# The last 512 rows of a scan as two chunks of 256, with their operands made in one piece

## The chip, the core and the metric

The kernel runs on one core of one Trainium2 chip. The metric is the device time of one launch in microseconds (us), the median of several runs. Engines are named as in the profile: PE is TensorE (with its weight loads as PEld), DVE is VectorE, ACT is ScalarE, POOL is GpSimd, SP is SyncE, whose queue issues most of the DMAs.

## The reference, cut to what matters

One layer on 4096 rows of 256 values, all in float32: a selective scan (Mamba) block with residual and layer norm, then a mixture of experts with residual and layer norm.

```python
x_in, z = split(x @ W_in.T)                       # 512 + 512 channels
xc = silu(causal_conv(x_in, 4 taps) + b_conv)
dt = softplus(xc @ W_dt.T + b_dt)
Bm, Cm = xc @ W_B.T, xc @ W_C.T                   # 16 states each
h = exp(dt * A) * h + dt * Bm * xc                # along the rows; 512 channels x 16 states
y = sum over states of h * Cm
x = layernorm(x + (y * silu(z)) @ W_out.T)
p = softmax(x @ router.T)                         # 32 experts; the 6 best of p + bias, weights renormed
out = sum over 6 of weight * down_e(silu(gate_e(x)) * up_e(x)) + shared expert(x)
x = layernorm(x + out)
```

## The kernel before, in words

**Chunks.** The rows go through in chunks of T = 512 (`SIZES`, `AT`, line 91): eight of them. For each chunk c there are three parts. `front(c)` (line 867) makes the scan's operands: input projection, convolution, silu, dt, the B and C rows (written to DRAM as `bcd`), and u times dt; inside it `gate(c-1)` (line 983) makes z of the chunk before. The scan itself is the loop over `units` (line 1223). `tail(c)` (line 1023) transposes the gated y, multiplies by W_out, adds the residual row, does the layer norm and calls `prepare(c)` (line 284): router, softmax, six best, `ranked` (line 411: each row's place in expert order, and the list of full tiles), and the shared expert.

**A unit of the scan** is 128 channels x 512 rows of one state: `du_at` multiplies u by the broadcast B row (POOL, line 1121), `exp_at` makes exp(dt A) in PSUM (ACT, line 1132), the scan runs over it (DVE, line 1260), its result is multiplied by the broadcast C row (DVE, line 1267) and summed over states by transposing matmuls into y (PE, line 1178). `keep` saves the last column as the next chunk's start (ACT, line 1159). There are 64 units a chunk, 512 in all. `load_bc` (line 1081) broadcasts a B or C row over 128 partitions, 256 KB, for two units at a time; B rows have 3 buffers, C rows 4. The du of a unit is issued four units ahead of its scan, the exponential two.

The helpers already have a short form, which nothing used so far: for a chunk below 512 rows (`short`, line 1068) a unit holds two channel blocks of 256 rows side by side in one 128x512 tile. Then there are 32 units a chunk, two exponentials a unit, `joined` (line 1138) folds the second block's start into du and sets that column of h to zero, and the loop calls `step` twice a unit.

**Order of the work.** Everything but the units is a Python generator in `threads`; `step()` advances every thread by one yield, once a unit (line 1279). So the order of each engine's instructions, and of SP's DMAs, is written out when the kernel is built, and every engine keeps to it. At a chunk's first unit (line 1225) the loop starts the threads of that chunk: the tail of the chunk before, the front of the chunk after (or, in the last chunk, `last_gate` and `walls`), `blanked` (zero rows for tiles to come). PSUM banks are held by `room` and `free`.

**Rows to experts.** `copies` (line 537) scatters each row block of a chunk six times into the DRAM buffer `xs`, which is ordered by expert (POOL, line 552, indirect DMA): 24 scatters for a chunk of 512. Between two scatters that directly follow each other it puts a small memset (line 550); before chunk NC - 2 it spreads them out instead. The row buffer is single: `load_rows` (line 1010) of a chunk waits for the scatters of the chunk before. A pair of full tiles of 128 rows is taken by `tiles` (line 706) as soon as a chunk's rows are placed; `full` (line 113) tells how many tiles a chunk completes. Of chunks before NC - 2 (`stage`, line 745) a pair is "own": it loads its two experts' weights itself (`loaded`, line 588, and `pair`, line 674). The later pairs run in `through_all` (line 1293) with all 32 experts resident in `wall`, a buffer that the scan's operands use before. `walls` (line 796) fills it in four steps: 18 experts' space is free at once, 4 more when the last gate is done, 5 when the scan is, 5 when the last chunk's output projection is. No resident pair starts before all are there. Each tile's result is added to one of three DRAM accumulators by an accumulating indirect DMA (POOL, line 664). When all are added, `finish` (line 1339) loads the three, adds them, does the layer norm and stores.

112 tiles are done by own pairs and 112 by resident pairs; before, 24 of the latter belong to chunk 6 and 88 to chunk 7.

Of the kernel before, what the change touches and what calls it, by code (L numbers as in the profile page):

```python
# [10 lines left out]
AF = mybir.ActivationFunctionType  # L11
# [5 lines left out]
P = 128  # L17
T = 512
NB = T // P
# [41 lines left out]
def kernel(  # L61
# [20 lines left out]
    nc = tc.nc  # L82
    L, D = x.shape
# [4 lines left out]
    NS = a_log.shape[1]  # L88
    TAPS = w_conv.shape[1]
    H = TAPS - 1  # L90
    SIZES = [T] * (L // T)
    NC = len(SIZES)
    AT = [sum(SIZES[:c]) for c in range(NC + 1)]
    E = router_t.shape[1]
# [21 lines left out]
    def blocks(c):  # L116
        return SIZES[c] // P

# [37 lines left out]
    threads = []  # L156
# [586 lines left out]
            yield  # L743

    def stage(c):
        own = c < NC - 2
        return [(c, j, own) for j in range(full[c - 1] if c else 0, full[c], 2)]


# [28 lines left out]
    scratch = cut(M, T)  # L778
    xin = cut(M, H + T)

    odd = (NC - 1) % 2
    us, dts, xTs = [None, None], [None, None], [None, None]
    us[1 - odd], dts[1 - odd], xTs[1 - odd] = cut(M, T), cut(M, T), cut(KD, T)
    bc_all = cut(T)
# [6 lines left out]
    z_all = cut(NB, DI)  # L791
# [27 lines left out]
    with ExitStack() as c1:  # L819
# [6 lines left out]

        def load_x(c):

            t = scratch.rearrange("p m t -> p (m t)")[:, : blocks(c) * D]
            t = t.rearrange("p (b d) -> p b d", d=D)  # L830
            nc.sync.dma_start(
                t, x[AT[c] : AT[c] + SIZES[c], :].rearrange("(b p) d -> p b d", p=P)
            )
            x_in[c] = t

# [28 lines left out]
        xT_of, u_of, z_of, dt_of, bcd_of, y_of = {}, {}, {}, {}, {}, {}  # L864
        b_of, c_of, du_of, h_of, hc_of = {}, {}, {}, {}, {}

        def front(c, gap):

            nb, Tc = blocks(c), SIZES[c]
            xT = xTs[c % 2]  # L870
            xT_of[c] = xT

            def turned(k):
                yield from room()
                pt = bank(f"pxt_{c}_{k}")
                for b in range(nb):
                    nc.tensor.transpose(pt[:, ts(b, P)], x_in[c][:, b, ts(k, P)], ident)
                yield
                nc.scalar.copy(xT[:, k, :Tc], pt[:, :Tc])
                free()  # L880

            yield from beside([turned(k) for k in range(KD)], 1)
            if c:
                last = SIZES[c - 1]
                nc.gpsimd.tensor_copy(xin[:, :, 0:H], xin[:, :, last : last + H])
            yield
            u = us[c % 2][:, :, :Tc]
            u_of[c] = u

            def projected(m):  # L890
                yield from room()
                px = bank(f"px_{c}_{m}")[:, :Tc]
                for k in range(KD):
                    nc.tensor.matmul(
                        px, w_in[:, k, ts(m, P)], xT[:, k, :Tc],
                        start=(k == 0), stop=(k == KD - 1),
                    )
# [36 lines left out]
            e = scratch[:, :, :Tc]  # L934
            dt_of[c] = dt

            def stepped(m):
                yield from room()
                pd = bank(f"pd_{c}_{m}")[:, :Tc]
                for k in range(M):  # L940
                    nc.tensor.matmul(  # L941
                        pd, w_dt[:, k, ts(m, P)], u[:, k, :],
                        start=(k == 0), stop=(k == M - 1),
                    )
                yield
# [12 lines left out]

            yield
            bcd = dram.tile([2 * NS, T], F32, tag="bcd", name=f"bcd_{c}")[:, :Tc]  # L960
            nc.sync.dma_start(bcd, bc)
            bcd_of[c] = bcd
            yield from beside([stepped(m) for m in range(M)], gap)

            for two in range(0, M, 2):
                yield
                while held[0] > len(pools) - 2:
                    yield
                lns = [bank(f"ln_{c}_{m}")[:, :Tc] for m in (two, two + 1)]
                for m, ln in zip((two, two + 1), lns):  # L970
                    nc.scalar.activation(ln, e[:, m, :], AF.Ln, bias=1.0)
                yield
                for m, ln in zip((two, two + 1), lns):
                    yield
                    nc.vector.tensor_add(ln, ln, dt[:, m, :])
                    nc.vector.tensor_mul(u[:, m, :], u[:, m, :], ln)
                    nc.scalar.copy(dt[:, m, :], ln)
                    free()
            if c + 1 < NC:
                yield from rounds(4)  # L980
                load_x(c + 1)

        def gate(c):

            while c - 1 not in z_done and c:
                yield
            z = z_all[:, : blocks(c)]
            z_of[c] = z

            def projected(b):  # L990
                yield from room()
                pz = bank(f"pz_{c}_{b}")
                for k in range(KD):
                    nc.tensor.matmul(
                        pz, xT_of[c][:, k, ts(b, P)], w_in[:, k, DI:],
                        start=(k == 0), stop=(k == KD - 1),
                    )
                yield
                nc.scalar.copy(z[:, b, :], pz)
                free()  # L1000

            yield from beside([projected(b) for b in range(blocks(c))], 2)

        def last_gate():
            yield from gate(NC - 1)
            yield
            nc.scalar.activation(z_of[NC - 1], z_of[NC - 1], AF.Silu)
            gated.add(NC - 1)

        def load_rows(c):  # L1010

# [211 lines left out]
        for q, (c, g, s, i) in enumerate(units):  # L1223
            left[c] -= 1
            if g == 0 and s == 0 and i == 0:
                mains = []
                if c == 0:
                    mains.append(blanks)
                else:
                    mains.append(tail(c - 1))  # L1230
                if c == 1:
                    mains.append(cleared())
                if c + 1 < NC:
                    mains.append(front(c + 1, 3))
                else:
                    mains.append(last_gate())
                    last_tail = tail(c)
                    threads.append(last_tail)
                if 0 < c:
                    ahead = blanked(bound(c - 1), bound(c), c)  # L1240
                if c == 2:
                    rest = tiles([item for c in range(NC) for item in stage(c)])
                    threads.append(rest)
                if c == NC - 1:
                    threads.append(walls())
                threads.extend(mains)

            if q % 4 == 0 and 0 < c:
# [169 lines left out]
```

## Time and profile before

| | us |
|---|---|
| median of 3 runs | 1851.69 (1851.32 to 1852.23) |
| profiled execution: time, span | 1859.8, 1857.9 |
| first units of chunks 4 to 7, at about | 741, 937, 1130, 1321 |
| last scan of the last chunk ends | 1508.3 |
| last accumulate lands | 1803.6 |
| busy in the span: PE, DVE, ACT, POOL | 1359.2, 1399.4, 990.9, 1216.3 |
| moved by DMA | 355.40 MB, 191 GB/s |

Groups of instructions that the change or its working touches (mean ns of one): scan 1283 and multiply by C 692 on DVE; du 1390 on POOL; exponential 128x512 692, tanh 128x512 586 and 128x256 384, state copy 158 on ACT; scatter 1001 and accumulate 1561 on POOL. One table load of ACT takes 1283.

How to read it: the page lists groups as line, engine, operation, output<-input, shape, count, then busy time, mean, idle time before them and what ended it. A timeline lists single instructions. In the DMA part "q1" is what the hardware queues of SP carry and "q0" what POOL's indirect DMAs carry; the share is the time their packets took on 16 engines. Busy shares are averages over stages; the windows show one stage at a time.

### The profile page before, as it was taken

The page shows a single profiled execution, that of the slowest core. Times are in us where ns is not written, and L with a number is a line of the kernel's source. Part 1 is how long each engine was busy: PE and PEld are TensorE (multiplying, and loading weights), DVE is VectorE, ACT ScalarE, POOL GpSimd, SP SyncE. Part 2 cuts the span into 40 slices and gives each one's busy share as a digit, 9 for nine tenths or more (in the row PEclk, how much of TensorE's full clock was granted, in tenths as well). Part 3 has the DMA queues.
Part 4 walks back from the last instruction along what each step waited for, and adds up shares of the span by engine and source line. Part 5 has one row for each costly group of instructions (what it writes and reads, how often), then busy time and mean ns, then how long its engine had stood idle before and what let it go on. Part 6 is the DMA issues. An engine that isn't in the chain of part 4 may idle for free. (4 is left out here: it accounts for less than half of the span.)

```text
span 1857.9 us, 24110 instructions
## 1 busy us (share of the span) xinstructions
PE 1359.2 (73%) x6208; PEld 944.8 (51%) x6208; DVE 1399.4 (75%) x2328; ACT 990.9 (53%) x2131; POOL 1216.3 (65%) x961
## 2 busy tenths in 40 slices
PE   8585696588669866986699668967775668699940
PEld 4242453355345545653566456645654566477730
DVE  1689989998998899779987998799979854122217
ACT  3676464547445755475557465756552333355533
POOL 0455644774585569665886599658956874878863
PEclk9796697779769887988989888988886987799975
DMA  8443692673469667875989589858998996599879
GB/s 238 136 126 102 219 307 77 164 212 123 94 192 257 166 160 177 251 206 126 258 215 263 131 234 245 236 139 214 271 257 236 260 268 100 123 145 144 144 131 306
DMA packets 318121, 355.40 MB, mean 191 GB/s; under 512 B 65056, under 2 KB 245024, under 8 KB 317984
## 3 DMA queue, kind: packets, MB, share of 16 engines
q1 hardware_dynamic: 274400, 296.02, 56.7%
q0 software_dynamic: 41472, 57.80, 17.3%
q8 instruction: 51, 0.84, 0.2%
q14 instruction: 86, 0.70, 0.1%
q10 hardware_dynamic: 2112, 0.05, 0.1%
HBM read 244.97 MB, written 108.77 MB: 190 GB/s over the span
## 5 line engine op out<-in xcount | busy, mean ns | idle before, releaser
L1121 POOL TENSOR_TENSOR du<-wall,bb 128x512 f32<-128x512 f32 x512 | 694.9, 1390 | 417.5 <-DVE h L1260 216.8
L1260 DVE TENSOR_TENSOR_SCAN h<-h,hlast,du 128x512 f32<-128x512 f32 x512 | 657.1, 1283 | 52.2 <-ACT hlast L1159 27.3
L1178 PE MATMUL y<-ident,hc 128*128 128x128 f32 x2048 | 345.2, 311 | 124.0 <-DVE hc L1267 104.0
L1132 ACT ACTIVATE h<-wall,aneg 128x512 f32<-128x512 f32 x512 | 353.7, 692 | 95.0 <-DVE hc L1267 80.4
L1267 DVE TENSOR_TENSOR hc<-h,cb 128x512 f32<-128x512 f32 x512 | 354.3, 692 | 58.6 <-DMA cb<-bcd 14.2
L1178 PEld LDWEIGHTS y<-ident,hc 128*128 128x128 f32 x2048 | 278.6, 162 | 233.9 <-DVE hc L1267 136.3
L552 POOL DMA_INDIRECT xs<-row,at x192 | 192.3, 1001 | 72.5 <-issue 39.2
L664 POOL DMA_INDIRECT acc<-ytl,no x112 | 174.8, 1561 | 59.4 <-issue 32.9
L664 POOL DMA_INDIRECT acc<-yt,no x112 | 177.5, 1585 | 53.2 <-ACT yt L658 28.7
L1159 ACT COPY hlast<-h 128x1 f32<-128x1 f32 x448 | 70.9, 158 | 260.7 <-DVE hc L1267 260.4
L1310 DVE SCALAR_TENSOR_TENSOR gt<-gt,pg 128x256 f32<-128x256 f32 x56 | 23.6, 421 | 175.5 <-ACT gt L1308 175.5
L682 PE MATMUL pg<-xsT,gu 128*128 128x128 f32 x896 | 123.8, 297 | 31.5 <-ACT xsT L644 25.4
L682 PEld LDWEIGHTS pg<-xsT,gu 128*128 128x128 f32 x896 | 118.0, 210 | 46.8 <-ACT xsT L644 29.5
L700 PE MATMUL po<-dn,hm 128*128 128x256 f32 x224 | 75.6, 469 | 83.5 <-DVE hm L694 35.6
L941 PE MATMUL pd<-wall 128*128 128x512 f32 x256 | 127.9, 649 | 9.5 <-DVE key L469 4.2
L905 PE MATMUL pv<-wall 128*128 128x512 f32 x256 | 117.4, 602 | 5.9 <-ACT hlast L1159 3.2
L1301 PE MATMUL pg<-wall,xsT 128*128 x448 | 113.0, 398 | 1.0 <-ACT xsT L644 1.0
L700 PEld LDWEIGHTS po<-dn,hm 128*128 128x128 f32 x224 | 46.9, 228 | 102.2 <-DVE hm L694 33.5
L641 PE MATMUL pt<-ident,xt 128*128 128x128 f32 x448 | 76.7, 298 | 24.1 <-DMA xt<-xs 21.2
L1301 PEld LDWEIGHTS pg<-wall,xsT 128*128 128x128 f32 x448 | 85.1, 200 | 12.3 <-ACT xsT L644 2.1
L941 PEld LDWEIGHTS pd<-wall 128*128 128x128 f32 x256 | 51.6, 211 | 66.8 <-issue 60.6
L641 PEld LDWEIGHTS pt<-ident,xt 128*128 128x128 f32 x448 | 61.0, 155 | 41.9 <-issue 25.3
(192 smaller groups left out, 1929.0 us busy)
## 6 DMA issues: line engine op xcount, KB each, us to landing
bb<-bcd SPq DMA_DIRECT2D x256, 256.0 KB
cb<-bcd SPq DMA_DIRECT2D x256, 256.0 KB
xs<-blank SPq DMA_DIRECT2D x55, 578.0 KB
xt<-xs SPq DMA_DIRECT2D x224, 128.5 KB
gu<-in_gate_up_t_dram SPq DMA_DIRECT2D x112, 256.0 KB
dn<-in_down_t_dram SPq DMA_DIRECT2D x112, 128.0 KB
wall<-acc SPq DMA_DIRECT2D x24, 512.0 KB
acc<-blank SPq DMA_DIRECT2D x16, 512.0 KB
```

Of the source, the lines that this page charges most:

```text
L552: i = nc.gpsimd.indirect_dma_start(out=xs, out_offset=bass.IndirectOffsetOnAxis(ap=at[:, b, k : k + 1], axis=0), in_=row[:, b, :], in_offs ...
L641: nc.tensor.transpose(pt4[:, i, k, :], xt[:, i, ts(k, P)], ident)
L664: a = nc.gpsimd.indirect_dma_start(out=acc[(j + i) % LANES], out_offset=bass.IndirectOffsetOnAxis(ap=no[:, i : i + 1], axis=0), in_=yt[:, ...
L682: nc.tensor.matmul(pg[:, h, i, :], gu[i][:, k, ts(h, P)], xT[:, i, k, :], start=(k == 0), stop=(k == KD - 1),)
L700: nc.tensor.matmul(po[:, i, :], hm[:, i, :], dn[i], start=True, stop=True)
L941: nc.tensor.matmul(pd, w_dt[:, k, ts(m, P)], u[:, k, :], start=(k == 0), stop=(k == M - 1),)
L1121: nc.gpsimd.tensor_mul(parts(q, du), u, row_for(q, 0))
L1132: nc.scalar.activation(h[:, ts(i, Tc)], dt_of[c][:, m + i, :], AF.Exp, scale=aneg[:, m + i, n : n + 1],)
L1178: nc.tensor.matmul(y_of[c, g][b // 2][:, b % 2, ts(m + j - 2 * g, P)], hc[:, ts(j * nb + b, P)], ident, start=(opens and j == 0 and b % 2 ...
L1260: nc.vector.tensor_tensor_scan(h, h, du_of.pop(q), hlast[:, n, m : m + 1], ALU.mult, ALU.add)
L1267: nc.vector.tensor_mul(parts(q, hc), parts(q, h), row_for(q, 1))
L1301: nc.tensor.matmul(pg[:, i].rearrange("p h t -> p (h t)"), xT[:, i, k, :], w, start=(k == 0), stop=(k == KD - 1),)
```

## The change

The last chunk of 512 becomes two of 256 (NC is now 9), each with its own scan, tail, ranking and list of tiles. `front` and `gate` still run once for both (FRONTS is 8): `of_parts` hands each short chunk its half. `last_gate` and `walls` start with the first of the two. Through `full` and `stage`, 24 resident tiles belong to chunk 6, 12 to chunk 7 and 76 to chunk 8; as NC - 2 is now 7, chunk 6's scatters are spread out as those of earlier chunks are. The number of units stays 512.

```diff
-    SIZES = [T] * (L // T)
+    SIZES = [T] * (L // T - 1) + [T // 2, T // 2]
+    FRONTS = L // T
...
     def stage(c):
-        own = c < NC - 2
+        own = c < FRONTS - 2
...
-    odd = (NC - 1) % 2
+    odd = (FRONTS - 1) % 2
...
+        def of_parts(t_of, c, t):
+
+            if c < FRONTS - 1:
+                t_of[c] = t
+                return
+            for i in range(2):
+                t_of[c + i] = t[..., ts(i, T // 2)]
...
         def front(c, gap):
-            nb, Tc = blocks(c), SIZES[c]
+            nb, Tc = NB, T
...
-            u_of[c] = u
+            of_parts(u_of, c, u)
...
-            dt_of[c] = dt
+            of_parts(dt_of, c, dt)
...
-            bcd_of[c] = bcd
+            of_parts(bcd_of, c, bcd)
...
-            if c + 1 < NC:
+            if c + 1 < FRONTS:
                 yield from rounds(4)
                 load_x(c + 1)
...
-            z = z_all[:, : blocks(c)]
-            z_of[c] = z
+            z = z_all
+            if c < FRONTS - 1:
+                z_of[c] = z
+            else:
+                z_of[c], z_of[c + 1] = z[:, : NB // 2], z[:, NB // 2 :]
...
         def last_gate():
-            yield from gate(NC - 1)
-            yield
-            nc.scalar.activation(z_of[NC - 1], z_of[NC - 1], AF.Silu)
-            gated.add(NC - 1)
+            yield from gate(FRONTS - 1)
+            yield
+            nc.scalar.activation(z_all, z_all, AF.Silu)
+            gated.update((NC - 2, NC - 1))
...
-                if c + 1 < NC:
+                if c + 1 < FRONTS:
                     mains.append(front(c + 1, 3))
+                elif c + 1 < NC:
+                    mains.append(last_gate())
+                    threads.append(walls())
                 else:
-                    mains.append(last_gate())
                     last_tail = tail(c)
                     threads.append(last_tail)
...
-                if c == NC - 1:
-                    threads.append(walls())
```

More of the change, by code (lines that the diff above doesn't have):

```diff
@@ L827, in load_x @@
         def load_x(c):
-            t = scratch.rearrange("p m t -> p (m t)")[:, : blocks(c) * D]
+            t = scratch.rearrange("p m t -> p (m t)")[:, : NB * D]
             t = t.rearrange("p (b d) -> p b d", d=D)
             nc.sync.dma_start(
-                t, x[AT[c] : AT[c] + SIZES[c], :].rearrange("(b p) d -> p b d", p=P)
+                t, x[AT[c] : AT[c] + T, :].rearrange("(b p) d -> p b d", p=P)
             )
@@ L883, in front @@
             if c:
-                last = SIZES[c - 1]
-                nc.gpsimd.tensor_copy(xin[:, :, 0:H], xin[:, :, last : last + H])
+                nc.gpsimd.tensor_copy(xin[:, :, 0:H], xin[:, :, T : T + H])
             yield
             u = us[c % 2][:, :, :Tc]
-            u_of[c] = u
+            of_parts(u_of, c, u)
             def projected(m):
@@ L1000, in projected @@
                 free()
-            yield from beside([projected(b) for b in range(blocks(c))], 2)
+            yield from beside([projected(b) for b in range(NB)], 2)
         def last_gate():
-            yield from gate(NC - 1)
+            yield from gate(FRONTS - 1)
             yield
-            nc.scalar.activation(z_of[NC - 1], z_of[NC - 1], AF.Silu)
-            gated.add(NC - 1)
+            nc.scalar.activation(z_all, z_all, AF.Silu)
+            gated.update((NC - 2, NC - 1))
         def load_rows(c):
```

## The prediction

> **What bounds the kernel now.** I read the page's 40 slices of time first, then the chain of waits backwards from the end, then cut the last two stages into windows. The last 512-row chunk is scanned from 1323 to 1508 us (64 units, a unit being one scan and one multiply by C); what follows is the tail of that chunk and the expert tiles. In the windows the columns are the window, its length, then busy us of PE, weight load, VectorE, ScalarE, GpSimd, then clock, DMA share and GB/s.
> ```profile
> 1320.90:1357.10 36.20, 21.91 (x133) 19.09 (x133) 33.69 (x40) 16.69 (x34) 34.31 (x27) 0.77 0.99 255
> 1357.10:1414.60 57.50, 42.55 (x216) 35.11 (x215) 43.69 (x81) 28.83 (x50) 32.28 (x25) 0.80 0.99 273
> 1414.60:1463.80 49.20, 30.14 (x154) 23.59 (x154) 46.39 (x95) 17.23 (x33) 35.89 (x31) 0.81 0.87 211
> 1463.80:1508.30 44.50, 27.37 (x165) 24.82 (x164) 33.51 (x40) 15.21 (x30) 40.18 (x33) 0.77 0.94 271
> ...
> 1592.00:1624.50 32.50, 14.62 (x68) 11.18 (x67) 3.29 (x8) 7.87 (x21) 26.68 (x24) 0.73 0.53 109
> 1624.50:1779.20 154.70, 146.42 (x752) 116.92 (x752) 35.35 (x84) 89.77 (x250) 125.04 (x81) 0.98 0.90 143
> ```
> The scan stage has no single bound: VectorE holds the first and third window (33.7 of 36.2, 46.4 of 49.2), DMA the second (share 0.99, VectorE idle 14 us), GpSimd the fourth. Who waits in the second window is seen in GpSimd's own timeline (in brackets the idle time before, and what ended it):
> ```profile
> 1362.83 2.50 POOL L1121 TENSOR_TENSOR du<-wall,bb 128x512 f32<-128x512 f32 x2 [5.06 <-DMA bb<-bcd]
> 1372.39 2.50 POOL L1121 TENSOR_TENSOR du<-wall,bb 128x512 f32<-128x512 f32 x2 [7.06 <-DMA bb<-bcd]
> 1377.10 2.51 POOL L1121 TENSOR_TENSOR du<-wall,bb 128x512 f32<-128x512 f32 x2 [2.20 <-DMA bb<-bcd]
> ```
> The broadcast rows of B come late because they stand in SP's queue behind expert tiles and resident weights: the scan is paced by bytes. After the scan PE looks like the bound, but PE stood still from 1592 to 1624; the waits there name the last chunk's scatter, and GpSimd's timeline shows a queue without gaps:
> ```profile
> PE pt L641 <- DMA xt<-xs: 12.8, 2, 12.3
> ```
> ```profile
> 1611.52 1.57 POOL L664 DMA_INDIRECT acc<-ytl,no  x1 [0.30 <-issue]
> 1613.39 0.98 POOL L552 DMA_INDIRECT xs<-row,at  x1 [0.30 <-issue]
> 1614.37 0.11 POOL L550 MEMSET between<- 128x1 f32 x1
> 1614.67 0.96 POOL L552 DMA_INDIRECT xs<-row,at  x1 [0.19 <-issue]
> 1615.94 1.60 POOL L664 DMA_INDIRECT acc<-ytl,no  x1 [0.30 <-issue]
> ```
> An add costs 1.87 us with its gap, a scatter 1.28, the memset between two scatters 0.3. The first add of a resident pair starts at 1551.9. 112 adds x 1.87 + 24 scatters x 1.28 + 8 memsets x 0.3 = 209 + 31 + 2 = 242 us, so 1794; the last add ended at 1799 and landed at 1803.6. So GpSimd's queue sets the end, not PE; 54.3 us of finishing (loads of the three accumulators, layer norm, stores) follow.
>
> **The change part by part.** The instruction order of the two built programs is the same up to the end of chunk 6's scan, front of the last 512 rows included; what differs lies after about 1320 us.
>
> (1) After the scan, taken away. Twelve of the 24 last scatters now stand inside the scan: 12 x 1.28 + 2 memsets = 16 us less of GpSimd's queue. The first add comes sooner: before, the last two halves of the output projection were interleaved with own pairs and ended at 1527.7, 19.4 us after the scan; now one half is left and no own pair: multiply 0.7, transposes and copies 2.2, projection 3.5, so some 8 us. The first rows landed 8 us later, at 1535.9; now they come behind the ten last resident experts (3.9 MB, 14 us at 271 GB/s from the scan's end, five of them let go only by the projection), so I take 12, and the first add follows 14 us after the first rows (before: 16, with twice the router in front of it on PE). That is 34 us after the scan against 43.6: 9.6 us, of which VectorE's ranking, about 2 us behind the add in the queue and hardly shorter for 256 rows, gives 2 back. The waits on positions in GpSimd's queue (3.5 us at 1558.8) shrink by about 3. Sum: -16 - 9.6 + 2 - 3 = -27; I take -28 with -24 and -33 as ends. The 33 us PE stall goes, but is worth no more than this: what is late next is GpSimd's queue of 112 adds, which ran on through the stall.
>
> (2) The scan of the two short chunks, bytes. The short chunks call the round-robin step twice a unit, so everything else in the stage is issued twice as densely. Counting in the built order what stands ahead of the broadcast row for the stage's 41st unit (unit 488 of 512): own expert tiles 14 before, 26 after (0.525 MB each by the issue table's sizes); resident experts 11 and 22 (0.393); blanking 4.0 and 2.4 MB; scatters 7 and 27 (0.148); adds 14 and 28 (0.131); broadcasts 10.5 MB in both; rows and shared sums 0.8 and 1.3. Sums: 29.8 and 44.2 MB. That row was queued from about 1305. At 273 GB/s (the second window) 44.2 MB take 162 us, at 291 (what 1460 to 1500 moved) 152; with GpSimd and VectorE behind it (about 8 us) unit 488 starts at 1465 to 1475, against 1446 before: +19 to +29, I take +24.
> The last 24 units took 62 us before. Now they hold only 24 x 1.98 = 47.5 us of scan and multiply, with hardly any tiles, but also the first short chunk's tail on VectorE: I add its rows with the sizes halved where they scale (layer norm 2, router 6, ranking 12, shared expert 1.5, sums 1.5) and get 23. 70.5 us at the 0.94 to 0.95 that VectorE reached in its windows is 75: +13, and +8 if it finds gaps; I take +11. Sum of the stage +27 to +42; I take +35.
>
> (3) The short form itself. A unit's exponential becomes two of 128x256. The rows: tanh 128x512 took 586 ns, 128x256 384, so 256 elements cost 202 and the halves are 692 - 202 = 490 each, +0.29 us. The Trainium skill's page "ScalarE: Activation LUTs" (Rules for kernel authors) speaks against such a split: about 0.3 us for each ACTIVATE plus 0.83 ns an element, so 0.51 each, +0.33. The joining of the two halves adds an Identity (nearest row: 128x4 square root, 205 ns) and a copy of one column (158 ns). With 0.04 for a wider state copy it is +0.69 us a unit by the rows, 44 us in 64 units; by the page, with 0.3 for each tiny one, 60. ScalarE was busy 78 us of the 187, so 122 to 138 with about 15 of tail and tiles lie beside 220: I cost it at nothing. VectorE's scan hides it, with exponentials and joins (1.6 us) needed two units (4 us) later. If that cover goes, the scan waits behind the join: ScalarE's excess over VectorE in the densest eight units (36 against 31 us), once or twice, 5 to 10 us. ScalarE's queue now also waits for du where only VectorE did; this is inside that figure. GpSimd's and VectorE's 128x2x256 forms have no row; the element count is the same, so 0, at most 5% of 1.28 us x 64 = 4; a gain is excluded as nothing is left out.
> B and C rows now travel in 1 KB pieces instead of 2 KB. The row: in chunk 0, 2,306 packets, nearly all broadcasts, held 32.0% of 16 engines for 40 us, 89 ns each, or 100 if the 256 short ones cost nothing; at the kernel's end 1 KB packets took 109.7% x 320 us / 7,278 = 48 ns, two of them 96. So between -4% and +8% on broadcasts worth 64 x 128 x 100 ns / 16 = 51 us: -2 to +4. The Trainium skill ("DMA: Bandwidth & Descriptors", Why small descriptors are slow) puts a fixed 3 cycles on each packet of 32-byte beats: 2 x 35 against 67 cycles, +4.5%, +2 us. I take +1, since the 1 KB row is at least as fast.
> Sum of (3): +1, from -2 to +12.
>
> (4) At nothing: gates and silu in one piece (same instructions), the earlier walls (bytes counted in 2), one more list of tiles, transposes into y (four a unit as before). Their cover is PE at 122 of 187 us in the stage; without it the half tail on PE would cost 14 us.
>
> Sum: -28 + 35 + 1 = +8. It is made on the profiled run, whose time is 1859.8 us (span 1857.9 and 1.9 around it), so 1867.8 there; the median of the runs is 1851.7, 0.996 of it, and +8 stays +8: **1859.7 us**.
>
> **The rivals.**
> *The scan stage absorbs the moved work* (not slower). Place: SP's queue between units 456 and 488. DMA's share is a sum over overlapping packets, it reached 1.10 at 362 GB/s at the end and 291 GB/s in a stretch with 13 scatters, so the extra 14 MB may move mostly beside VectorE. For it: up to unit 488 VectorE's own sum is 40 x 1.98 + 31 of tail + 14 pairs x 0.84 = 122 us, GpSimd's 40 x 1.3 + 28 x 1.75 + 27 x 1.19 = 133. Against it: in the mixed second window DMA gave 273 at share 0.99 while GpSimd starved. Price: stage +12 to +20 instead of +36, so -16 to -8, about 1840. It decides from a lengthening of less than 28 us, i.e. from about 310 GB/s up to unit 488 or a later part that finds VectorE's gaps.
> *Both cancel*: stage +25 to +31: 1848 to 1855.
> *ScalarE becomes the scan's bound or queues lock* (much slower): steps twice as dense leave PE, ScalarE and VectorE half the units between a product and its reader; each own pair then holds VectorE's queue (one such wait of 2.7 us at 1365 before). At 1 us for each of 13 pairs in the dense part and 10 for the join: +31 in all, 1882 at worst, 1872 for the middle.
> *The change doesn't do what it says*: excluded by the built order: twelve scatters do stand before the last scan.
>
> **How the numbers follow.** Forecast, slower by 4 to 14 us: 0.48. Absorbed, faster: 0.25. Cancelling: 0.15. Locked queues: 0.12. A measurement of this kernel tells about 0.2% (3.7 us) from no change. So faster 0.25, same 0.15, slower 0.60. Range: 1836 to 1878, which leaves the best half of the absorbed case and the worst of the locked one out. The likeliest case's own range is 1855 to 1866.
>
> **What would show it.** Scan of the last unit ending 36 us later than 1508 in the span; DMA share near 1 and GpSimd waiting for bb between units 456 and 488; the rest of the stage at VectorE 0.95. After the scan: first resident add at +34, 12 scatters, no PE stall before the last tiles, add after add at 1.87 us until about +266, then 54 us. Wrong if the stage ends within 25 us of before, if ScalarE exceeds VectorE in the stage, or if the adds' period changes.

## The result, and the profile after

The changed kernel takes 1899.55 us (median of 4 runs, 1894.86 to 1904.12) against 1851.96 for the kernel before on the same chip: ratio 1.0248, 95% interval 1.0225 to 1.0272. It is slower, as forecast, but by 47.6 us and not by 8, and lies outside the range of 1836 to 1878.

The profiled execution has a span of 1897.4 us against 1857.9, 39.5 more. Three stretches make that sum, cut at the starts of the scans of unit 447 (the last of the chunk before) and unit 511 (the last of all):

| stretch | before | after | difference | forecast |
|---|---|---|---|---|
| up to unit 447 | 1318.2 | 1321.8 | +3.6 | 0 |
| units 447 to 511, "the stage" | 188.8 | 260.2 | +71.4 | +36 |
| unit 511 to the end of the last add | 293.9 | 258.2 | -35.7 | -28 |
| finish | 57.0 | 57.2 | +0.2 | 0 |

Each stretch comes from one profiled execution. The 3.6 us ahead of unit 447, where both programs have the same order, show how much two executions can differ. The profiled execution of before is one of its longer ones (1859.8 us; the median is 1851.96). The kernel before with one more buffer (e18 below, ratio 1.0006) gives 187.3 us for its stage and 286.8 after it, in a span of 1851.3. Against that trace the stage grew by 72.9 and the gain after the scan is 28.6, not 35.7. So the gain came, and in the size forecast or up to 8 us more; the stage grew twice as much as forecast.

First the windows of the kernel before, cut at units 447, 487 and 511 (columns as in the prediction: length, busy us of PE, weight load, VectorE, ScalarE, GpSimd, clock, DMA share, GB/s):
```profile
1318.20:1442.00 123.80, 79.72 (x420) 66.87 (x418) 106.11 (x194) 54.44 (x101) 85.96 (x67) 0.77 0.93 251
1442.00:1507.00 65.00, 42.30 (x243) 35.27 (x241) 52.44 (x63) 24.56 (x49) 58.04 (x48) 0.84 0.97 256
```
The changed kernel at the same units, and its time after the scan:
```profile
1321.80:1501.90 180.10, 121.39 (x630) 99.53 (x631) 113.91 (x215) 100.68 (x286) 119.71 (x94) 0.82 0.93 243
1501.90:1582.00 80.10, 36.58 (x159) 29.94 (x158) 70.21 (x133) 41.39 (x110) 51.30 (x48) 0.65 0.57 136
1582.00:1843.00 261.00, 218.38 (x1082) 173.36 (x1082) 65.32 (x198) 126.20 (x350) 186.62 (x128) 0.93 0.79 133
```
In the last 24 units VectorE is busy 70.2 of 80.1 us: the half tail that the change brings into the scan, as forecast. In the first 40 units VectorE's own work grew by 7.8 us (106.1 to 113.9) and the time by 56.3: it stands idle 66.2 us in place of 17.7. No engine is near full there, and the DMA share is the 0.93 of before, at nearly the same rate; PE has 630 matmuls in place of 420. This idle time is what the prediction lacks.

VectorE's waits in the stage (in total, times, longest) name who ends it:
```profile
DVE gt L695 <- ACT gt L692: 42.1, 10, 13.1
DVE base L403 <- DMA acc<-base: 15.1, 1, 15.1
DVE mx L323 <- PE pr L316: 4.2, 1, 4.2
```
Before, gt waited once:
```profile
DVE gt L693 <- ACT gt L690: 2.7, 1, 2.7
```
The longest of the waits after is followed here through three queues, in excerpts from their timelines. PE:
```profile
1351.39 0.41 PE L643 MATMUL pt<-ident,xt 128*128 128x128 f32 x2 [4.78 <-DMA xt<-xs]
1353.48 0.69 PE L643 MATMUL pt<-ident,xt 128*128 128x128 f32 x2 [1.68 <-DMA xt<-xs]
1354.81 5.55 PE L1065 MATMUL px<-wall,gyt 128*128 128x256 f32 x16
1360.20 1.88 PE L1007 MATMUL pz<-wall 128*128 128x512 f32 x4
1361.92 1.95 PE L684 MATMUL pg<-xsT,gu 128*128 128x128 f32 x16
```
ScalarE:
```profile
1354.20 0.59 ACT L646 COPY xsT<-pt 128x512 f32<-128x512 f32 x1 [3.64 <-PE pt L643]
1362.12 0.59 ACT L1012 COPY wall<-pz 128x512 f32<-128x512 f32 x1 [5.51 <-PE pz L1007]
1363.90 0.38 ACT L692 ACTIVATE gt<-pg 128x256 f32<-128x256 f32 x1 [1.20 <-PE pg L684]
```
VectorE:
```profile
1349.92 1.28 DVE L1273 TENSOR_TENSOR_SCAN h<-h,hlast,du 128x512 f32<-128x512 f32 x1
1364.32 0.42 DVE L695 SCALAR_TENSOR_TENSOR gt<-gt,pg 128x256 f32<-128x256 f32 x1 [13.12 <-ACT gt L692]
1365.11 0.68 DVE L1280 TENSOR_TENSOR hc<-h,cb 128x512 f32<-128x512 f32 x1
```
A tile's rows (xt) land late and stop PE for 6.5 us; the tail's projection px and the gate's pz are next in PE's order, 7.4 us of work, and only then comes the pair's own product pg. VectorE stood 13.1 us before gt; the multiply by C of the scan at 1349.92 stands behind it in the order. One late load has passed through three queues into the scan, and the work that stands between in PE's order has about doubled it.

After the scan the first add starts 29.3 us after the last scan's end (before: 43.6; forecast 34), and the queue goes on as before, an add or a scatter after the other at the same periods:
```profile
1612.57 1.62 POOL L666 DMA_INDIRECT acc<-ytl,no  x1 [36.74 <-ACT hT L1333]
1614.49 1.00 POOL L554 DMA_INDIRECT xs<-row,at  x1 [0.30 <-DVE fend L485]
1615.80 1.59 POOL L666 DMA_INDIRECT acc<-ytl,no  x1 [0.30 <-ACT ytl L660]
1617.70 0.99 POOL L554 DMA_INDIRECT xs<-row,at  x1 [0.30 <-issue]
```
The PE stall of 12.8 us for the scattered rows (xt) has shrunk to this line of PE's waits after the scan:
```profile
PE pt L643 <- DMA xt<-xs: 0.9, 1, 0.9
```

### The profile page after: what moved, and what is told of

It is laid out like the page before. It is cut to its first block, busy times and chain, and to the rows that moved or that the text cites. A ratio compares the mean times of both kernels' runs of the same rounds, so it can differ in the third digit from the quotient of the medians.

```text
span 1897.4 us, 24491 instructions
## 1 busy us (share of the span) xinstructions
PE 1371.6 (72%) x6230; PEld 953.8 (50%) x6230; DVE 1416.8 (75%) x2395; ACT 1043.3 (55%) x2364; POOL 1216.6 (64%) x963
## 5 line engine op out<-in xcount | busy, mean ns | idle before, releaser
L1191 PE MATMUL y<-ident,hc 128*128 128x128 f32 x2048 | 350.3, 314 | 145.4 <-DVE hc L1280 111.0
L1145 ACT ACTIVATE h<-wall,aneg 128x512 f32<-128x512 f32 (+1 forms) x576 | 370.9, 644 | 41.5 <-DVE hc L1280 24.2
L666 POOL DMA_INDIRECT acc<-ytl,no x112 | 174.4, 1557 | 74.6 <-ACT hT L1333 38.9
L660 ACT ACTIVATE ytl<-po,wt 128x256 f32<-128x256 f32 x112 | 47.0, 471 | 66.9 <-DMA acc<-ytl,no 61.5
## 6 DMA issues: line engine op xcount, KB each, us to landing
bb<-bcd SPq DMA_DIRECT2D x256, 256.0 KB
cb<-bcd SPq DMA_DIRECT2D x256, 256.0 KB
gu<-in_gate_up_t_dram SPq DMA_DIRECT2D x112, 256.0 KB
```

Source lines behind the costliest of these rows:

```text
L666: a = nc.gpsimd.indirect_dma_start(out=acc[(j + i) % LANES], out_offset=bass.IndirectOffsetOnAxis(ap=no[:, i : i + 1], axis=0), in_=yt[:, ...
L1145: nc.scalar.activation(h[:, ts(i, Tc)], dt_of[c][:, m + i, :], AF.Exp, scale=aneg[:, m + i, n : n + 1],)
L1191: nc.tensor.matmul(y_of[c, g][b // 2][:, b % 2, ts(m + j - 2 * g, P)], hc[:, ts(j * nb + b, P)], ident, start=(opens and j == 0 and b % 2 ...
```

## The experiments

They ran later and on chips where the kernel before took 1855 to 1864 us, so ratios to the runs of before beside them are compared, and stretches inside the traces. "Stage" and "after" are the second and third stretch above, VectorE's busy and idle time are those of the stage; then come the time of the stage's first 40 units, the MB that moved in them and PE's matmuls there. The ratios' intervals reach 0.1 to 0.3% to either side. A stretch is that of one execution: pairs of kernels with the same time (before and e18, the changed kernel and e4) differ in their traces by 1.5 and 0.2 us in the stage, by 7.1 and 2.4 after it, so differences of a few us tell nothing.

| run | ratio | stage | VectorE busy, idle | first 40 units: us, MB, matmuls | after |
|---|---|---|---|---|---|
| before | 1 | 188.8 | 158.5, 30.3 | 123.8, 31.1, 420 | 293.9 |
| after | 1.0248 | 260.2 | 184.1, 76.1 | 180.1, 43.7, 630 | 258.2 |
| e1_gate_only | 1.0104 | 196.8 | 157.9, 38.9 | 126.6, 28.0, 447 | 298.8 |
| e2_long_two_steps | 1.0171 | 226.3 | 158.5, 67.8 | 177.2, 45.6, 626 | 284.9 |
| e3_tiles_one_step | 1.0085 | 225.6 | 179.2, 46.4 | 142.4, 31.6, 449 | 266.3 |
| e5_walls_late | 1.0184 | 253.6 | 185.1, 68.5 | 171.1, 36.0, 628 | 265.3 |
| e6_pairs_one_step | 1.0159 | 256.0 | 183.8, 72.2 | 170.2, 40.4, 541 | 261.4 |
| e13_pairs_once_walls_late | 1.0126 | 239.9 | 181.5, 58.4 | 150.2, 32.4, 543 | 263.1 |
| e14_tile_loads_twice | 1.0162 | 250.3 | 182.3, 68.0 | 160.9, 36.2, 544 | 260.6 |
| e15_walls_twice | 1.0039 | 226.7 | 180.4, 46.3 | 145.0, 35.5, 457 | 259.9 |
| e16_more_c | 1.0181 | 252.9 | 184.1, 68.8 | 172.2, 43.2, 628 | 255.9 |
| e17_walls_twice_more_c | 1.0019 | 220.9 | 180.2, 40.7 | 137.3, 35.1, 456 | 259.8 |

**Is it the dense steps, or the short form with its join?** Four edits; theory 1 of their texts is that the dense steps hold the queues up. e1: the second step of a unit is left out, but for the gate and the tail beside it until the gate is done (the second chunk's units need it).
```diff
-    def step():
-        threads[:] = [g for g in threads if alive(g)]
+    def step(only=None):
+        threads[:] = [g for g in threads if (only and g not in only) or alive(g)]
...
-            if short(c):
-                step()
+            if short(c) and c not in gated:
+                step(mains)
```


> The changed kernel with one step a unit in the short chunks; only the tail and the last gate get a second step, and only until the gate is done. If the doubled steps cost the time (theory 1: every engine's queue meets its producer on another engine too soon), the scan stage falls from about 262 us back to 200 to 215 and the total lies at 1850 to 1870. If the short form costs it (theory 2: ScalarE's split exponentials and joins hold the scan), the stage stays above 240 and the total above 1885. If the bytes moved into the stage cost it (theory 3), the stage is about 205, as no tiles are moved.

e2: the kernel before, its last chunk in the long form, with two steps a unit.
```diff
-            if short(c):
+            if c + 1 == NC:
                 step()
```


> The kernel before, long form, with two steps a unit in the last chunk. Theory 1: the scan stage grows from 190 to 225 to 250, total 1870 to 1895. Theory 2: the stage stays at about 190 and the part after it is shorter by the own pairs' backlog, total 1840 to 1850. Theory 3 (bytes): the stage grows by 20 to 30, total 1855 to 1870.

e3: the second step leaves out the tiles' loads, the pairs and the resident weights; tail, gate and scatters keep it.
```diff
+    once = []
...
-    def step():
-        threads[:] = [g for g in threads if alive(g)]
+    def step(second=False):
+        threads[:] = [g for g in threads if (second and g in once) or alive(g)]
...
+                once.append(going[-1])
...
+                    once.append(threads[-1])
...
+                    once.append(rest)
...
-                step()
+                step(True)
```


> The changed kernel, but expert tiles and resident weights get one step a unit as before; tail, gate and scatters keep two. Theory 1: the scan stage is 205 to 225, the part after it about 20 us shorter than before, total 1855 to 1875. Theory 2: stage above 240, total above 1885. Theory 3: as theory 1, and DMA no longer near full in the first short chunk.

e4: the changed kernel without the join, so that the second block of a unit starts from the first block's last column, which is not the reference's start.
```diff
-            if q >= len(units) or not short(units[q][0]):
-                return
+            return
```


> The changed kernel without the join: the second block of a unit starts from the first block's last column (that part of the computation is changed). Takes 64 x 0.5 us from ScalarE and the link GpSimd to ScalarE to VectorE. Theory 2: the total falls by 25 us or more, to 1875 or less. Theory 1: it falls by 0 to 10, 1890 to 1900. Theory 3: by 0 to 5.

e4 gave 1.0225 (1.0207 to 1.0242) and a stage of 260: 126 instructions less on ScalarE change it by nothing that can be told. (The totals in these four texts count from a kernel before of 1852 us; on their chip it took 1862.) e1 has the short form with nearly single steps: +8 us. e2 has neither short chunks nor a half tail, and its stage still grew by 37.5 us, all of it idle time of VectorE, which stands 30.8 us in nine waits for gt and 22.2 in one for base:
```profile
DVE gt L693 <- ACT gt L690: 30.8, 9, 13.3
```
So the density of the steps makes the idle time, with or without the short form. But e2 does not tell how: its first 40 units also moved 45.6 MB in place of 31.1, and for most of them the DMA share was 1.00:
```profile
1327.30:1460.00 132.70, 91.93 (x486) 74.46 (x486) 87.23 (x181) 52.49 (x106) 91.86 (x78) 0.87 1.00 250
```
At the 251 GB/s of before, 45.6 MB take 182 us; the 40 units took 177.2. e2 is as theory 3, the bytes, would have it, but for the size that its text gave.

e1 also shows what the halving alone is worth after the scan: nothing (298.8); it is the doubled stepping of the tail (e3: 266.3) that brings the half tail into the scan, and 21 us of VectorE's work with it (157.9 to 179.2).

From e1 to e3 the idle time grows by 7.5 us, from e3 to the changed kernel by 29.7: the tiles and weights at two steps are the costly part, and they buy 8 us after the scan. e3 also speaks against bytes as all of it: it moved the 31 MB of before in its first 40 units, and they took 18.6 us longer.

**Bytes, locks, or one wait?** In what follows theory A says that loads packed into fewer microseconds pace the dense units, theory B that PE, ScalarE and VectorE hold each other up in order.

e5: the weights start with the second short chunk.
```diff
                     mains.append(last_gate())
+                else:
                     threads.append(walls())
-                else:
                     last_tail = tail(c)
```


> The changed kernel with one line moved: the router's and expert's resident weights (8.65 MB of loads, with their matmuls px, pz and copies) start with the second short chunk and not with the first, so the 40 dense units after unit 447 carry that much less. Theory A (bytes: the stage grew because the loads of the last chunks fall into fewer microseconds) expects the stretch from unit 447 to 511 to fall from 260 us by 20 or more, the total to about 1.00 to 1.01 of the kernel before. Theory B (locks: matmul, ScalarE, VectorE and back, in queues that run in order, with half as many units between a product and its reader) expects the stretch to fall by 0 to 10 us, and the time after the scan to grow by 0 to 10 as some weights come late: ratio 1.02 to 1.03.

Its first 40 units:
```profile
1321.40:1492.50 171.10, 120.15 (x628) 97.50 (x629) 113.97 (x214) 100.51 (x286) 119.77 (x94) 0.84 0.86 210
```
They moved 36.0 MB and not 43.7, 18% less, at 210 GB/s and not 243, and took 171.1 us and not 180.1. Theory A falls as the sole cause: with the changed kernel's rate the time would have been 148. That bytes are no limit at all does not follow: with the weights gone another limit, close behind, can hold the time at 171.

e6: as e3, but only `once.append(going[-1])` stays, so the pairs alone are at one step.

> The changed kernel with the expert pairs' compute (transposes pt, product pg, gate gt) stepped once a unit in the short chunks, while their loads, the resident weights and the tail stay at two steps: about the same bytes as early as in the changed kernel, but the chain pt, xsT, pg, gt only half as dense. Theory B (locks) expects VectorE's wait of 42 us for gt to fall under 15 and the stretch from unit 447 to 511 from 260 us to 235 or less; the pairs left over cost about 5 to 10 after the scan: ratio about 1.01. Theory A (bytes) expects the stretch within 10 us of 260 and a ratio of 1.02 or more.

VectorE's waits in e6's stage:
```profile
DVE base L405 <- DMA acc<-base: 15.2, 1, 15.2
DVE row L1076 <- DMA row<-in_x_dram: 13.7, 2, 8.3
DVE row L1076 <- PE px L1068: 9.1, 1, 9.1
DVE gt L697 <- ACT gt L694: 8.3, 3, 6.3
```
The wait for gt fell from 42.1 to 8.3 us, as theory B has it, and the stage by only 4: waits of the tail for its rows (row) and for its projection (px) came in its place. Theory B in its simple form falls too. The first 40 units, 170.2 us for 40.4 MB (237 GB/s, share 0.92), are near the pace of before for bytes.

e7: the second shared-expert sum gets its own buffer, against the single wait of 15.1 us.
```diff
-            base = q1.tile([P, T], F32, tag="sg", name=f"base_{c}_{h}")
+            base = q1.tile([P, T], F32, tag=("sg", "base")[h], name=f"base_{c}_{h}")
```


> The changed kernel with the shared expert's second sum in a buffer of its own, so that VectorE's sum need not wait until the first one has been added to the output in memory (15.1 us once in the short chunks, after's wait of base for acc). If that wait is on the path, the stretch from unit 447 to 511 falls by 10 to 15 us and the ratio to about 1.017. If other waits end as late (the loads, the locks), it falls by under 4 and the ratio stays at 1.023 to 1.027.

Ratio 1.0238; the wait is gone, gt waits 54.1 us in place of 42.1, the stage is 263.2. e8 puts this on e3, and `FRONTS - 2` for `NC - 2` in `copies`, so that chunk 6's scatters aren't spread.

> Three mends of the changed kernel together: tiles, pairs and resident weights stepped once a unit (tail, gate and scatters twice), the second sum in its own buffer, and the scatters of the last whole chunk sent without the spacing of the scan, so that the last tail may begin sooner. By the sum of the parts: the stretch from unit 447 to 511 about 208 us (225.7 with the first mend, less about 10 for the buffer, less about 8 for the spacing), after the scan about 266: ratio 0.995, 0.99 to 1.005. If the waits only move to the loads, the stretch stays at 220 to 226 and the ratio at 1.006 to 1.01.

Ratio 1.0074, stage 222.3 for 225.6, after the scan 267.3: the two additions are worth 0.1%, which the intervals don't tell from nothing.

**A ring through SyncE's queue?** Its waits in the changed kernel's stage (L1104 are the loads of B and C rows, which wait until the scan frees their buffers; the tiles' loads stand behind them):
```profile
SPq L1104 <- DVE hc L1280: 41.5, 8, 14.5
SPq L1104 <- POOL du L1134: 30.9, 10, 7.1
```
Theory C: the scan waits for gt, gt for a tile's load, the load behind a C row's load that waits for the scan. Four runs issued the loads of B and C rows on ScalarE's queue, e9 those of the short chunks alone, e10 all, e11 all in the kernel before, e12 all in e8. All four also have a 4-byte load on SyncE's queue after each blanking store, which was not tried alone. The cut shows one of the two places in e10 to e12; e9 has `(nc.scalar if short(c) else nc.sync)` there:
```diff
-                nc.sync.dma_start(
+                nc.scalar.dma_start(
```


> The changed kernel with the short chunks' loads of B and C rows (bb, cb) issued on ScalarE's queue and not on SyncE's (and a 4-byte load after each blanking store, which costs nothing). In the changed kernel SyncE's queue stood 41.5 us for hc and 30.9 us for du between unit 447 and 511, the times at which the scan's next B and C rows found no free buffer; the pairs' and weights' loads stood behind them. Theory C (a ring: loads wait for the scan in SyncE's queue, the scan waits for the gate gt in VectorE's, the gate waits for those loads) expects the stretch from unit 447 to 511 to fall from 260 us to 225 or less and the ratio to 1.01 or less. Theory B (the lock is among TensorE, ScalarE and VectorE alone) and theory A (bytes) expect it at 250 or more and a ratio of 1.02 to 1.025.

> As the run before, but the loads of B and C rows of all chunks are issued on ScalarE's queue. If the ring binds only where the steps are dense, the time up to unit 447 stays within 5 us of the changed kernel's 1322, and the ratio is that of the run before. If ScalarE's queue is held up by the loads' own waits, the time up to unit 447 grows by 10 us or more.

> The kernel before with the loads of B and C rows of all chunks on ScalarE's queue. Its SyncE queue stood 31.4 us for hc and du in the last chunk, and VectorE nearly nothing for gt (2.7 us). Theory C expects no ring there, so a ratio of 0.99 to 1.003; if the loads on ScalarE's queue delay its exponentials, 1.005 or more.

> The version with the three mends (tiles, pairs and weights once a unit, second sum apart, scatters of the last whole chunk quick), and the loads of B and C rows on ScalarE's queue. Its stretch from unit 447 to 511 was 222 us, with 53 us of SyncE's queue standing for hc and du. Theory C expects 205 to 215 and a ratio of 0.995 to 1.003; theories A and B no change, 1.007.

They gave 1.0277, 1.0592, 1.0329 and 1.0505; e9's stage is 266.5. None of the expected gains came, and the test is spoiled by what it puts on ScalarE: an issue takes 0.33 us there, as in this line of e11, and the exponentials stand behind it: VectorE waited for them 68.1 us in the whole of e11 and 18.4 in the kernel before.
```profile
1002.00 0.33 ACTq L1097 DMA_DIRECT2D cb<-bcd  x1
```
In e11 unit 447 comes at 1376.9 us and not 1318.2. So theory C is neither shown nor refuted by these four. The last group asks again with one more buffer for C rows, the load left where it is:
```diff
-                bufs=3 + which,
+                bufs=3 + 2 * which,
```


> The changed kernel with five buffers and not four for the C rows (cb), so that their loads find a free buffer two units sooner and SyncE's queue need not stand for hc (41.5 us in the changed kernel between unit 447 and 511). If the standing makes the idle time of VectorE, the stretch falls from 260 us to 240 or less and the ratio to 1.015 or less. If the standing only shows that the scan is late, the stretch stays within 8 us and the ratio at 1.021 to 1.027.

> The version with tiles and pairs at one step a unit and everything else at two, with five buffers for C rows. If the standing of SyncE's queue matters (38.7 us for hc there), the stretch falls from 227 us to 215 or less and the ratio from 1.004 to 0.998 or less; if not, 1.002 to 1.006.

> The kernel before with five buffers for C rows. Its SyncE queue stood 12.9 us for hc in the last chunk. If that costs the scan anything, the ratio is 0.997 or less; if not, 0.998 to 1.002.

SyncE's waits in e16's stage:
```profile
SPq L1104 <- POOL du L1134: 47.4, 13, 7.7
SPq L1104 <- DVE hc L1280: 12.5, 8, 3.3
```
The standing for hc fell by 29 us; that for du grew by 16.5, the stage fell by 7.3. e16 gave 1.0181, 0.7% better than the changed kernel; e18, the kernel before with the same buffer, 1.0006 (0.9990 to 1.0022). So the standing costs something where the steps are dense, and nothing that can be told before; it is a tenth of the growth, and e16's ratio lies between the two forecasts of its text. In e16 the first 40 units moved 43.2 MB at 251 GB/s and a share of 0.97. e17 (on e15) is the best of the mended versions, 1.0019 (1.0007 to 1.0031): its stage fell by 5.8 us and not to 215, and it is still not faster than before.

**Which density?** Three runs between e3 and the changed kernel: e13 is e5 and e6 together (the weights' thread stands behind the tail's, in e5 before it); e14 and e15 are e3 without `once.append(rest)` (the tiles' loads back at two steps) and without `once.append(threads[-1])` (the weights).

> The changed kernel with the pairs' compute at one step a unit and the resident weights started with the second short chunk; the tiles' loads and the tail stay at two steps. Each of the two edits alone left the stretch from unit 447 to 511 at 254 and 256 us. If the two densities each suffice to keep it long and it takes both to shorten it, it falls to 235 or less and the ratio to 1.010 or less. If the dense loads of the tiles keep it long, it stays at 245 or more and the ratio at 1.014 to 1.018.

> The version with tiles, pairs and weights at one step a unit (stretch 225.7 us, VectorE idle 46 of it), with the tiles' loads alone back at two steps. If the loads' order and bytes make the 30 us of idle time, the stretch goes back to 245 or more, ratio 1.015 or more; if the pairs and weights do, it stays within 8 us of 226, ratio 1.006 to 1.011.

> The same version with the resident weights alone back at two steps. If the weights' density makes the idle time once the tail is dense, the stretch goes from 225.7 to 240 or more, ratio 1.014 or more; if not, it stays within 8 us, ratio 1.006 to 1.011.

e13 fell between its two forecasts, 239.9 us and 1.0126. Its two edits together took 20.3 us off the changed kernel's stage, where alone they took 6.6 (e5) and 4.2 (e6). e15: the weights at two steps cost the stage 1 us, though its first 40 units then moved 35.5 MB instead of 31.6; the ratio, 1.0039, is below its forecast because the time after the scan fell by 6.4. e14: the tiles' loads at two steps cost 24.7. Their windows up to unit 487, e3 first, then e14:
```profile
1326.40:1468.80 142.40, 89.38 (x449) 71.33 (x449) 109.55 (x201) 90.29 (x257) 101.30 (x82) 0.77 0.86 222
```
```profile
1320.20:1481.10 160.90, 102.61 (x544) 83.44 (x544) 113.80 (x208) 96.23 (x273) 110.63 (x88) 0.82 0.89 225
```
The 36.2 MB of e14 are hardly more than e15's 35.5, which took 145.0 us; what differs is the tiles: 87 more matmuls and 11 us more of GpSimd's work than in e15, because a pair begins when its loads are there. No single wait of VectorE carries the 18.5 us from e3 to e14. GpSimd's wait for the scan's B rows grew, over the whole stage in e3 and then in e14:
```profile
POOL du L1137 <- DMA bb<-bcd: 15.4, 4, 7.8
```
```profile
POOL du L1137 <- DMA bb<-bcd: 25.4, 8, 10.1
```
In the first 40 units alone that wait was 4.2 us once and 24.0 in seven pieces. That is as much as the 18.5, but VectorE's own rows name no wait for du of that size.

Over the runs with a dense tail and these loads on SyncE (the table's, e4, e7 and e8), the time of the first 40 units goes with the tile work in them: 449 to 472 matmuls 137 to 151 us, 541 to 544 matmuls 150 to 170, 628 to 633 matmuls 171 to 183. Within the middle group the bytes count as well: 32.4 MB (e13), 36.2 (e14) and 40.4 (e6), by when the weights come, took 150, 161 and 170 us, 2.5 us for 1 MB; with sparse tiles 3.9 MB cost 2.6 us (e3 to e15).

**Two limits close together?** Bytes and tile work mostly rise together, so the runs part them only in places. At the 251 GB/s of before, the bytes moved in these 40 units would take 174 us in the changed kernel (measured 180), 172 in e16 (172), 182 in e2 (177) and 161 in e6 (170): there bytes at the mean pace of before come near to the whole time. They would take 143 in e5 (measured 171), 144 in e14 (161), 129 in e13 (150) and 126 in e3 (142): there something else holds. So the runs also agree with two limits close behind each other, the bytes and the in-order work of the tiles, of which removing one leaves the other; e13, where both edits gave twice the sum of each alone, speaks for this. It was read from the runs afterwards and not tested by one of its own.

Some of the tiles moved forward are won after the scan, but few: in the whole stage 15 pairs are computed after and 12 before, and 32 adds are done in place of 24.

## Why the prediction was wrong, point by point

**(1) After the scan, -28: right in its mechanism; -35.7 against the trace of before, -28.6 against that of e18.** The first add came 14.3 us sooner after the last scan than in the trace of before, 8.0 than in that of e18 (forecast 9.6). From it to the end of the last add took 227.7 us, against 249.0 and 248.2: some 21 less (forecast 17: 16 for twelve scatters, 3 for waits, 2 given back). GpSimd's queue is the bound as foreseen: its 124 adds and scatters follow each other at a median of 1.86 us, as before. Two readings were off without harm. PE did not stand still for 33 us: its row for 1592.00 to 1624.50 has 14.62 us of work, and the wait for the scattered rows was 12.8. And the 1799 of the last add is its start; it ends at 1800.9.

**(2) The stage, +35: the step that failed.** "At 273 GB/s (the second window) 44.2 MB take 162 us, at 291 (what 1460 to 1500 moved) 152" takes bytes as the only pace of the first 40 units, at the rate of a good window. The count of bytes was about right (43.7 MB moved). The rate was not: 243 GB/s, where the same 40 units of before had reached 251. The prediction's own count shows it for the kernel before: 29.8 MB from 1305 to the row of unit 488, eight us ahead of 1446, is 133 us or 224 GB/s. At that rate 44.2 MB take 197 us, so the units come 64 us later and not 24. Measured is +56.3, 7.8 of it VectorE's own work and 48.5 its idle time. That the better rate comes near is in part luck, since bytes are not the only pace: with 18% fewer of them the units still took 171.1 us (e5), and with the bytes of before 142.4 (e3, 123.8 before). The last 24 units were right: VectorE 70.5 us forecast, 70.2 measured; at a busy share of 0.88 and not 0.94 to 0.95, +15.1 for +11.

What VectorE stood for was named, in the rival *ScalarE becomes the scan's bound or queues lock*, and priced "At 1 us for each of 13 pairs". The waits for gt alone were 42.1 us in ten pieces, 4.2 each. That price took the single wait of 2.7 us of a sparse order and made it smaller; in e2, where the steps are as dense, the same wait is 30.8 us in nine pieces. Its cure by the pairs alone does not work either (e6): once the order is dense, other waits take the place.

**(3) The short form, +1: not refuted.** e1's stage is 8.0 us longer, with the gate's dense steps in it, e4 finds the join worth nothing measurable. Sizes, from the groups of the changed kernel's stage (mean ns after the busy us):
```profile
L1145 ACT ACTIVATE h<-wall,aneg 128x256 f32<-128x256 f32 x126 | 60.2, 478 | 27.3 <-DVE hc L1280 24.2
L1159 ACT ACTIVATE du<-h,du,hlast 128x1 f32<-128x1 f32 x63 | 22.2, 352 | 22.5 <-POOL du L1134 17.7
```
A half exponential takes 478 ns (490 by the rows, an estimate of 510 by the rule of the Trainium skill's page "ScalarE: Activation LUTs", Rules for kernel authors). The joining Identity takes 352, where the square root's row gave 205 and the rule's fixed part about 300: here the rule was the nearer. The copy of one column takes 163: there the row (158) was. So a unit costs ScalarE 0.78 us more and not 0.69, still hidden, as ScalarE is busy 142 of 260 us. The +1 for the shorter pieces of the B and C rows was not measured by itself.

**(4) At nothing.** The weights' second step costs the stage 1 us beside sparse tile loads (e3 to e15) and 5.7 beside dense ones (e14 to e6); there their earlier start, with one step, costs 10.4 more (e13 to e14). The other items were not tried one by one.

**The rivals.** *Absorbed* and *cancel* fall with the stage at +71. The locked queues had the direction, but of their two parts ScalarE as the bound did not come (142 us busy against VectorE's 184), and their worst price, 1882, was still short. Of the signs to watch, the DMA share was 0.93 and not near 1. GpSimd's wait for bb in the stage was as large as before (16.7 against 16.0 us); it is a poor sign of bytes, since in e2, at a share of 1.00, it was 15.5.

**What stays open.** That the density of the steps makes the idle time, and of them that of the tiles and weights the larger part, is shown (e1, e2, e3). That the form and the join do not make the bulk of it, and bytes alone not all of it, is shown too (e1, e4, e5, e14). How much of it is bytes at the pace of before and how much the order of the tile work isn't settled, nor through which wait it acts: each wait taken away alone (gt in e6, base in e7, hc in SyncE's queue in e16) gave 4, -3 and 7 us of 71, the others moved up. That late loads and in-order queues take part is seen in single stalls such as the one above; the share of each is not separated.

## What to carry to other kernels

Where one program order drives all engines, the distance between a product and its reader is a resource: halving it for work that isn't urgent can cost the loop even where the bytes leave room (e5: 171 us for what would be 143 at the old rate). So make dense only what must come sooner (here the tail, worth 32 us after the scan for 29 of the stage) and leave the rest at its pace (tiles and weights: 8 us for 35). When a bound is read from one good window, put the same count to the whole stage of the old kernel first: here that alone would have turned +24 into +64. And price a wait that the old order hardly shows by an order that shows it, not by its one small row.

## What the runs showed of the hardware that was not expected

Single waits replace each other almost without loss: 18% fewer bytes in the dense units (e5), 34 us less of the wait for gt (e6), 29 us less of SyncE's standing for hc (e16) moved the stage by 6.6, 4.2 and 7.3 us. The first two together (e13) moved it by 20.3. The issue of a broadcast on ScalarE takes 0.33 us of its queue, and with all of them there unit 447 came 58.7 us later (e11, which also has the 4-byte loads). A one-column Identity on ScalarE, with scale and bias from memory, takes 352 ns, a one-column copy 163.
